# Mamba layer of a three-layer kernel: z's projections, their SiLU, rounding terms and copies in other slots; five buffers for products with C, four each for B and C, C fetched two slots later

## The chip, the cores and the metric

The kernel runs on one core of a Trainium2 chip. TensorE (PE) multiplies matrices into PSUM, VectorE (DVE) does elementwise work and scans, ScalarE (ACT) does activations and copies, GpSimd (POOL) does elementwise work in SBUF, and SyncE (SP) issues most of the DMA transfers. Each engine works through its own instructions in the order in which the program gives them, and waits on semaphores for the others. The metric is the device time of one execution in microseconds (us). The kernel before takes 4107.07 us, the median of 3 runs (4106.33 to 4110.94).

## The reference, cut to what matters

Three layers run one after another on 4096 tokens of 256 channels: a hybrid of convolutions and attention, a bidirectional Mamba layer with a small MLP, and a mixture of experts. The change touches the Mamba layer alone. For each direction (forward, and backward over the reversed tokens) it computes:

```python
xz = einsum('bld,ed->ble', x, in_proj_w);  xc, z = split(xz, 2)      # 512 channels each
xc = silu(depthwise_conv4(xc) + conv_b)
x_dbl = einsum('bld,ed->ble', xc, x_proj_w)                          # dt: 16, B: 16, C: 16
dt = softplus(einsum('blr,dr->bld', dt, dt_proj_w) + dt_proj_b)
h_t = exp(dt_t * A) * h_{t-1} + dt_t * B_t * xc_t                    # 512 channels x 16 states
y_t = sum_s h_t[s] * C_t[s]
y = (y + xc * Dp) * silu(z)
out = y @ out_proj_w.T
```

Forward and backward are added, normalised, put through a leaky MLP, and added to the input; a second LayerNorm makes the input of the third layer.

## The kernel before, in words

**Chunks and slots.** The 4096 tokens are cut into 8 pieces of N = 512. Each piece is worked on once per direction, which makes 16 *chunks* i = 0 to 15; even i is forward (d = 0), odd i is backward (d = 1). A chunk is worked through in 32 *slots* (`SPS`): a slot (e, k, j) holds 128 partitions by 2 x 512 values, that is 64 channels with four of their 16 states each. Within a chunk the slot's number is at = 8e + 2k + j/2, with e = 0..3 (a quarter of the channels), k = 0..3 (a quarter of the states), j = 0 or 2. All 512 slots go through the loop at L2022.

**What a slot does.** In the loop's order, for slot n:

- POOL: `inflow(n + 2)` (L1928) multiplies dt·xc by B into a tile `dbx` (three buffers).
- ACT: `keep(n - 1)` (L1977) copies the last state of the scan before; `decay(n + 1)` (L1918) makes exp(dt·A) for the next slot in a PSUM tile `da` (two buffers), with two activations; `bring(n + 1)` (L1971) adds the state brought in from the chunk before to the next `dbx`. For slots 1, 9, 17 and 24 (`LONG`) POOL does that (L1969).
- DVE: `recur(n)` (L1941) is the scan h = da·h + dbx over 1024 values, and `readout(n)` (L1951) at the end of the slot multiplies the result by C into a tile `h` (pool `hp`, four buffers).
- In seven slots, `POOLED` = {0, 4, 8, 12, 16, 20, 28}, the scan writes straight into a buffer of `h`, and the product with C is made by POOL one slot later (`pooled(n - 1)`, L1956), so DVE has no readout there.
- PE: `sum_states` (L1986) sums `h` over the states into a PSUM tile `y`, for two slots (a pair) at once. A pair that begins at an even slot m is summed in slot m + 2, or in slot m + 3 where m is in `POOLED`. That sum is what sets the pair's two buffers of `h` free.
- DVE: `close` (L1995), in slots 1, 9, 17 and 25, multiplies y by silu(z).

**What runs beside it.** `prepare(q)` is a Python generator that makes chunk q's inputs during the chunk before (from slot 27 of the one before that); one step of it is taken in each slot. In a steady chunk its steps fall so: in slots 3 to 7 the convolution; slot 8 the SiLU of xc with a table load on either side (L1392, and L1331 in `exp_and_log`); slot 9 the projection to dt, B and C (L1398); slot 10 its copy `xd` (L1402) and the write to `bcd`; slots 11 to 15 the projection of dt (L1423) with Abs and Relu (L1419, L1420); slot 16 an Exp; from slot 17 the softplus by quarters: `rounding(e)` (two ACT operations, L1432 and L1433), `total(e)` (PE, L1438), `logs(e)` (ACT Ln, L1441), a last matmul (L1471), `keep_dt(e)` (ACT copy, L1444); and in slots 21, 23, 25, 27 `dt_piece` (POOL, L1496, then two DMA writes of dt and dt·xc, L1500). z is made by `z_of(q, e)` (PE, L1342, four matmul instructions for each e) and copied from PSUM by `keep_z(q, e)` (ACT, L1486): quarters 0 and 1 in slots 9 to 11, quarters 2 and 3 in slots 19 to 22. All these PE results share two PSUM buffers (`mm`). z's SiLU (L2062, two activations between two table loads) comes in slot 0 of the chunk that uses it.

`tail(c)` is another generator, for the LayerNorms and the MLP of two finished chunks. It begins in slot 3 of an even chunk and takes at most one step a slot; each step says which engine it needs next (`needs`), and slots listed for that engine in `FULL` are passed over. So `FULL` sets in which slots the tail's work falls, over the next two chunks.

**Loads.** SP issues, in the order of the loop, `load_bc(i + 1, k)` in slots 24, 26, 28 and 30 (L1529: B and C of quarter k, 256 KB each, spread over the partitions from DRAM, in tiles `b` and `c` of pool `bcp`, five buffers each) and `load_dt` (L1539: dt and dt·xc, 512 KB each) in slots 3, 5, 11, 13, 19, 21, 27 and 29 for the e that follows. The tail's LayerNorms write and read small rows through DRAM on the same queue (L138, L140, L145, L146).

Of the kernel before, what the change touches and what calls it, by code (L numbers as in the profile page):

```python
# [30 lines left out]
NCH = NT // N  # L31
# [6 lines left out]
ET = DI // P  # L38
DS = 16
DR = 16  # L40
SQ = DS // 4
# [1214 lines left out]
def mamba_phase(cx, early, w_in, w_x, w_out, w1, w2, x1d, ud, bcd, dtd, x2d, u2d, usum):  # L1256
# [11 lines left out]
    nc, tc = cx.nc, cx.tc  # L1268
    with ExitStack() as ctx:
        one = ctx.enter_context(tc.tile_pool(name="c_one", bufs=1))  # L1270
        pr = ctx.enter_context(tc.tile_pool(name="c_pr", bufs=2))
        sp = ctx.enter_context(tc.tile_pool(name="c_sp", bufs=1))
        bcp = ctx.enter_context(tc.tile_pool(name="c_bc", bufs=5))
        dtp = ctx.enter_context(tc.tile_pool(name="c_dt", bufs=3))
        up = ctx.enter_context(tc.tile_pool(name="c_u", bufs=3))
        hp = ctx.enter_context(tc.tile_pool(name="c_h", bufs=4))
        ip = ctx.enter_context(tc.tile_pool(name="c_i", bufs=2))
        tl = ctx.enter_context(tc.tile_pool(name="c_tl", bufs=1))
        pda = ctx.enter_context(tc.tile_pool(name="c_pda", bufs=2, space=PSUM))
# [12 lines left out]
        for d in range(2):  # L1292
            for lst, have, src, shape, nm in (
# [6 lines left out]
                t_ = one.tile(shape, FP, name=f"{nm}{d}")  # L1300
# [59 lines left out]
        def prepare(q):  # L1360

            d, got = q % 2, gots[q]

            ps = in_pair(q, 0)
            yield
            yield
            xp = early.wide("xp")
            nc.scalar.copy(xp[:, :, 0:3], halo[d])
            for v in range(2):
                nc.scalar.copy(xp[:, v, 3:], ps[v])  # L1370
            ps = in_pair(q, 2)
            yield
            yield
            for v in range(2):
                nc.scalar.copy(xp[:, 2 + v, 3:], ps[v])
            nc.scalar.copy(halo[d], xp[:, :, N : N + 3])
            for _ in range(4):
                yield

            xc = None  # L1380
            for e in range(ET + 1):
                if e > 0:
                    xc = got["xc"] = xc or pr.tile([P, ET, N], FP, name="xc", tag="xc")
                    nc.scalar.activation(xc[:, e - 1, :], ps, AF.Identity, bias=cx.col(f"convb{d}", e - 1))
                if e < ET:
                    ps = mm_psum()
                    for k in range(4):
                        nc.tensor.matmul(  # L1388
                            ps, taps[d][:, 4 * e + k, :], xp[:, e, k : k + N], start=k == 0, stop=k == 3
                        )  # L1390
                yield
            nc.scalar.activation(xc, xc, AF.Silu)  # L1392
            exp_and_log()
            yield
            ps = mm_psum()
            nx = DR + 2 * DS
            for e in range(ET):
                nc.tensor.matmul(ps[0:nx, :], wx[d][:, e, :], xc[:, e, :], start=e == 0, stop=e == ET - 1)  # L1398
            z_of(q, 0)
            yield  # L1400
            xd = few()[0:nx, :]
            nc.scalar.copy(xd, ps[0:nx, :])  # L1402
            keep_z(q, 0)
            z_of(q, 1)

            at = 0 if d else DR
            nc.sync.dma_start(out=bcd[q], in_=xd[at : at + 2 * DS, :])
            yield


            r = slice(32 * d, 32 * d + DR)
            ex = dt = None
            for e in range(ET + 1):
                if e == 0:
                    keep_z(q, 1)
                if e > 0:
                    ex = early.wide("ex")[:, :, 0:N] if e == 1 else ex
                    dt = got["dt"] = dt or sp.tile([P, ET, N], FP, name="dt", tag="dt")
                    nc.scalar.activation(ex[:, e - 1, :], ps, AF.Abs, bias=cx.col(f"dtb{d}", e - 1))  # L1419
                    nc.scalar.activation(dt[:, e - 1, :], ps, AF.Relu, bias=cx.col(f"dtb{d}", e - 1))  # L1420
                if e < ET:
                    ps = mm_psum()
                    nc.tensor.matmul(ps, wdt[r, P * e : P * e + P], xd[r, :], start=True, stop=True)  # L1423
                yield

            nc.scalar.activation(ex, ex, AF.Exp, scale=-1.0)
            yield
            rds, sums = {}, {}

            def rounding(e):  # L1430
                rds[e] = few()
                nc.scalar.activation(rds[e], ex[:, e, :], AF.Identity, scale=-1.0, bias=-1.0)  # L1432
                nc.scalar.add(rds[e], rds[e], 1.0)  # L1433

            def total(e):
                sums[e] = mm_psum()
                for v, x in enumerate((rds.pop(e), ex[:, e, :], dt[:, e, :])):
                    nc.tensor.matmul(sums[e], cx.ident, x, start=v == 0, stop=False)  # L1438

            def logs(e):  # L1440
                nc.scalar.activation(ex[:, e, :], ex[:, e, :], AF.Ln, bias=1.0)  # L1441

            def keep_dt(e):
                nc.scalar.copy(dt[:, e, :], sums[e])  # L1444
                if q < 2:
                    return
                h = e // 2
                if e % 2 == 0:
                    firsts[q, h] = ip.tile([P, 2], FP, name="first", tag="first")
                nc.scalar.copy(firsts[q, h][:, e % 2 : e % 2 + 1], sums[e][:, 0:1])  # L1450
                if e % 2:
                    first_rows[q, h] = cx.rows.tile([P, 2], FP, name="first_row", tag="first_row", bufs=2)
                    nc.sync.dma_start(out=first_rows[q, h], in_=firsts[q, h])

            rounding(0)
            yield
            for e in range(ET + 1):
                if e > 0:
                    keep_dt(e - 1)
                if e < ET:  # L1460
                    total(e)
                if e < ET - 1:
                    rounding(e + 1)
                if 0 < e < 3:
                    keep_z(q, e + 1)
                yield
                if e < ET:
                    logs(e)
                    if e < 2:
                        z_of(q, e + 2)  # L1470
                    nc.tensor.matmul(sums[e], cx.ident, ex[:, e, :], start=False, stop=True)  # L1471
                if e > 0:
                    dt_piece(q, 1, e - 1)
                if e == 1 and q + 1 < 2 * NCH:
                    load_u(q + 1)
                if e == ET and q > 1:
                    load_first(q, 0)
                yield

        def z_of(q, e):  # L1480
            zs[e] = in_proj(q % 2, gots[q]["u"], ET + e)

        def keep_z(q, e):
            if e % 2 == 0:
                gots[q].setdefault("z", []).append(sp.tile([P, 2, N], FP, name="z", tag="z", bufs=3))
            nc.scalar.copy(gots[q]["z"][e // 2][:, e % 2, :], zs.pop(e))  # L1486
# [33 lines left out]
                old = state[q % 2].rearrange("p (e a b) k -> p e a b k", a=2, b=2)[:, tiles, :, 1, :]  # L1520
                nc.gpsimd.tensor_tensor(brought[q, h], brought[q, h], old, ALU.mult)

        def load_bc(i, k):

            tiles = []
            for nm, r in (("b", 0), ("c", DS)):
                t_ = bcp.tile([P, N], FP, name=nm, tag=nm)
                rows = bcd[i][r : r + DS, :].rearrange("(s k) n -> k s n", s=4)[k]
                nc.sync.dma_start(out=t_, in_=rows[None].to_broadcast([32, 4, N]))  # L1529
                tiles.append(t_)  # L1530
            bcs[i, k] = tiles

        def load_dt(i, e, j):

# [373 lines left out]
        gots, bcs, dts, m_of, das, us, ys, hs = {}, {}, {}, {}, {}, {}, {}, {}  # L1908
# [25 lines left out]
        def recur(n):  # L1934
# [3 lines left out]
            h = hs[n] = hp.tile([P, 2, N], FP, name="h", tag="h")  # L1938
            if n % SPS in POOLED:
                das[n] = h  # L1940
# [52 lines left out]
        def close(i, e):  # L1993
# [4 lines left out]
        CARRY = {30: (0, 0), 31: (0, 2), 9: (1, 0), 11: (1, 2)}  # L1998


        POOLED = {0, 4, 8, 12, 16, 20, 28}

        AHEAD = 5

# [1 line left out]
        LONG = {1, 9, 17, 24}  # L2006

        FULL = {
            "PE": {1, 2, 3, 4, 5, 6, 7, 9, 18, 20, 21, 22, 24, 27, 29},
            "ACT": {0, 6, 7, 8, 9, 14, 15, 16, 20, 22, 30, 31},  # L2010
            "POOL": {1, 5, 9, 13, 17, 21, 23, 25, 27, 29, 30, 31},
            "DVE": {8, 11, 16, 24},
            "DMA": {},
        }
        needs = ["PE"]
        with tc.manual_schedule(engines=ORDERED):
# [5 lines left out]
            for n, (i, e, k, j) in enumerate(slots):  # L2022
                at = n % SPS
# [8 lines left out]
                    decay(n + 1)  # L2032
                bring(n + 1)
                recur(n)
                nxt = (i, e + 1) if e < ET - 1 else (i + 1, 0)
                if nxt[0] < 2 * NCH:
                    if e == ET - 1 and j == 0:
                        load_bc(i + 1, k)
                    if (k, j) == (1, 2):
                        load_dt(*nxt, 0)  # L2040
                    if (k, j) == (2, 2):
                        load_dt(*nxt, 2)
# [11 lines left out]
                if 1 <= at <= 3 and out is not None:  # L2054
                    step(out)
                    if at == 3:
                        out = None
                        if (i - 1) % 2:
                            tails.append(tail((i - 1) // 2))
                if at == 0 and i > 0:  # L2060
                    for z in gots[i]["z"]:
                        nc.scalar.activation(z, z, AF.Silu)  # L2062
                    exp_and_log()
                if i == 0:
# [376 lines left out]
```

## Time and profile before

| | us |
|---|---|
| median of 3 runs | 4107.07 |
| the profiled execution: device time | 4108.35 |
| the profiled execution: span of its instructions | 4106.5 |
| Mamba's scans: first starts, last ends | 1930.3, 3815.0 |
| DVE busy, whole span | 3456.2 (84%) |
| PE busy, whole span | 3577.7 (87%) |
| ACT busy, whole span | 2640.9 (64%) |
| POOL busy, whole span | 1814.7 (44%) |
| between 2000 and 3700 us (1700 us): DVE, POOL, PE, ACT busy | 1579.3, 1457.6, 1422.4, 1294.4 |

The profiled execution lies 1.28 us above the median, and its device time 1.85 us above its span. The profile lists for each line of the kernel the instructions it made, their mean duration, and the engine's idle time just before them with what ended it. `da`, `h`, `dbx`, `y`, `z`, `mm` and so on are tile names. A chunk's beginning can be read from the timeline as the start of its first scan: chunk 5 begins at 2521.3 us, chunk 6 at 2641.7, chunk 7 at 2755.0, chunk 8 at 2877.4. Below, "slot 5.12" is slot 12 of chunk 5.

### The profile page before, as it was taken

The numbers are of one execution on the slowest core, as the hardware profiler recorded it, in microseconds if no ns is written. First come the engines' busy times: TensorE is split into PE (matmuls) and PEld (weight loads), VectorE is DVE, ScalarE is ACT, GpSimd is POOL, SyncE is SP. The second block draws the span as 40 slices with busy tenths as digits, with TensorE's granted clock in tenths as the row PEclk, the third lists the DMA queues.
The fourth block names the chain that finished last, engine by engine and source line by source line (L and its number), as shares of the span: only waits on it lengthen the run. The fifth ranks groups of instructions, "written<-read, shape, count | busy, mean of one in ns | idle before, by whom it ended". The sixth has DMA issues, their size and how long they took to land. (4 is left out here: it accounts for less than half of the span.)

```text
span 4106.5 us, 43589 instructions
## 1 busy us (share of the span) xinstructions
PE 3577.7 (87%) x14968; PEld 1200.4 (29%) x14968; DVE 3456.2 (84%) x2887; ACT 2640.9 (64%) x4233; POOL 1814.7 (44%) x1193
## 2 busy tenths in 40 slices
PE   6769888999999999997788888888888988786898
PEld 2224332222222222222222223222322323222344
DVE  8998777989889889877899999998999999899322
ACT  1111226888888888875678777787877778775222
POOL 3020000000000000002888888888888889898100
PEclk9889998999999999998889999898999989897999
DMA  6232215223222323214333344434334334432121
GB/s 208 94 103 92 80 58 158 51 61 64 66 61 57 66 63 65 50 41 143 121 101 117 113 132 121 136 121 122 109 103 136 122 124 132 132 113 88 56 63 55
DMA packets 164325, 399.95 MB, mean 97 GB/s; under 512 B 36997, under 2 KB 46469, under 8 KB 163838
## 3 DMA queue, kind: packets, MB, share of 16 engines
q1 hardware_dynamic: 137166, 304.26, 23.9%
q0 software_dynamic: 24624, 84.43, 8.9%
q10 hardware_dynamic: 2304, 8.39, 0.6%
q8 instruction: 119, 1.95, 0.2%
q14 instruction: 112, 0.92, 0.1%
HBM read 268.17 MB, written 79.56 MB: 85 GB/s over the span
## 5 line engine op out<-in xcount | busy, mean ns | idle before, releaser
L1928 POOL TENSOR_TENSOR dbx<-dtxr,b 128x1024 f32<-128x1024 f32 x512 | 1202.6, 2358 | 225.5 <-DMA dtxr<-dtd 99.5
L1044 ACT ACTIVATE e<-sc 128x1024 f32<-128x1024 f32 x1024 | 993.7, 1023 | 165.5 <-PE sc L1037 143.0
L1941 DVE TENSOR_TENSOR_SCAN da<-da,state,dbx 128x1024 f32<-128x1024 f32 x400 | 938.9, 2347 | 58.5 <-ACT dbx L1971 17.4
L954 DVE TENSOR_TENSOR s<-s,e 128x1024 f32<-128x1024 f32 x768 | 880.2, 1216 | 19.7 <-ACT e L1044 19.0
L1918 ACT ACTIVATE da<-dtr,aneg 128x512 f32<-128x512 f32 x1024 | 707.9, 691 | 34.5 <-DMA dtr<-dtd 3.1
L1037 PE MATMUL sc<-q,kS 32*128 32x512 f32 x4096 | 648.7, 646 | 15.7 <-ACT e L1044 11.4
L961 PE MATMUL av<-e,vT 128*32 128x512 f32 x4096 | 551.8, 609 | 0.1
L1951 DVE TENSOR_TENSOR h<-da,c 128x1024 f32<-128x1024 f32 x400 | 488.5, 1221 | 22.9 <-PE mm L1423 1.4
L977 POOL DMA_DIRECT2D s<-s x94 | 81.5, 874 | 942.3 <-DVE s L954 856.8
L462 PE MATMUL cv<-v,u 128*128 128x512 f32 x928 | 413.5, 606 | 28.3 <-DVE pad L283 14.2
L1986 PE MATMUL y<-h,sel 128*32 128x512 f32 x2048 | 335.8, 629 | 95.0 <-DVE h L1951 77.2
L1037 PEld LDWEIGHTS sc<-q,kS 32*128 32x128 f32 x4096 | 211.0, 184 | 455.8 <-issue 254.0
L1941 DVE TENSOR_TENSOR_SCAN h<-da,state,dbx 128x1024 f32<-128x1024 f32 x112 | 262.5, 2343 | 53.6 <-PE y L1986 44.1
L1956 POOL TENSOR_TENSOR h<-h,c 128x1024 f32<-128x1024 f32 x112 | 263.9, 2357 | 28.9 <-ACT state L1977 28.8
L1342 PE MATMUL mm<-u,win 128*128 128x512 f32 x464 | 237.7, 654 | 30.7 <-ACT xp L1370 28.1
L462 PEld LDWEIGHTS cv<-v,u 128*128 128x128 f32 x928 | 179.1, 195 | 260.5 <-issue 228.1
L560 DVE SCALAR_TENSOR_TENSOR acc<-pad,wdw_s,acc 128x768 f32<-128x768 f32 (+1 forms) x192 | 235.9, 1233 | 19.9 <-ACT acc L553 14.2
L1977 ACT COPY state<-da 128x2 f32<-128x2 f32 x399 | 63.1, 158 | 280.8 <-DVE h L1951 279.4
L1388 PE MATMUL mm<-xp,taps 128*128 128x512 f32 x480 | 214.1, 598 | 0.0
L143 POOL TENSOR_TENSOR ln_few<-ln_few,minus_half 128x4 f32<-128x4 f32 x29 | 32.1, 1106 | 398.4 <-DMA ln_few<-ln_row 259.5
L954 DVE TENSOR_TENSOR s<-e 128x1024 f32<-128x1024 f32 x128 | 152.0, 1217 | 59.2 <-ACT e L1044 50.3
L961 PEld LDWEIGHTS av<-e,vT 128*32 128x32 f32 x4096 | 81.7, 108 | 394.4 <-issue 386.7
(381 smaller groups left out, 3910.8 us busy)
## 6 DMA issues: line engine op xcount, KB each, us to landing
dtr<-dtd SPq DMA_DIRECT2D x128, 512.0 KB
dtxr<-dtd SPq DMA_DIRECT2D x128, 512.0 KB
s<-s POOLq DMA_DIRECT2D x94, 512.0 KB, 6.0
b<-bcd SPq DMA_DIRECT2D x64, 256.0 KB
c<-bcd SPq DMA_DIRECT2D x64, 256.0 KB
dtd<-dt SPq DMA_DIRECT2D x64, 256.0 KB
dtd<-few SPq DMA_DIRECT2D x64, 256.0 KB
u<-uv SPq DMA_DIRECT2D x24, 640.0 KB
```

Source lines behind the costliest of these rows:

```text
L462: nc.tensor.matmul(rows4(ps), u[:, dy, P * ci : P * ci + P], v[:, dy : dy + HR, ci, :], start=dy + ci == 0, stop=dy == k - 1 and ci == CT - 1,
L954: nc.vector.tensor_tensor(z, x, y, ALU.add)
L961: nc.tensor.matmul(g.av[32 * h : 32 * h + 32, :], vT[:, kb, P * t + 32 * h : P * t + 32 * h + 32], es[h // 2][:, h % 2, :], start=kb == 0, ...
L1037: nc.tensor.matmul(ps[h // 2][:, h % 2, :], kS[r, t, P * kb : P * kb + P], q_t[r, t, :], start=True, stop=True,)
L1044: nc.scalar.activation(e, ps[i], AF.Exp)
L1342: nc.tensor.matmul(ps, win[d][:, t, P * e : P * e + P], u[:, t, ::-1] if d else u[:, t, :], start=t == 0, stop=t == CT - 1,)
L1918: nc.scalar.activation(da[:, v, :], dts[i, e, j][0][:, v, :], AF.Exp, scale=aneg[i % 2][:, a : a + 1])
L1928: nc.gpsimd.tensor_tensor(u, dts[i, e, j][1], bcs[i, k][0][:, None, :].to_broadcast([P, 2, N]), ALU.mult)
L1941: nc.vector.tensor_tensor_scan(das[n].rearrange("p v n -> p (v n)"), da.rearrange("p v n -> p (v n)"), u.rearrange("p v n -> p (v n)"), st ...
L1951: nc.vector.tensor_tensor(hs[n], das[n], bcs[i, k][1][:, None, :].to_broadcast([P, 2, N]), ALU.mult)
L1956: nc.gpsimd.tensor_tensor(hs[n], hs[n], bcs[i, k][1][:, None, :].to_broadcast([P, 2, N]), ALU.mult)
L1986: nc.tensor.matmul(ys[i, e][32 * j : 32 * j + 32, :], cx.sel, hs[n + j // 2][:, j % 2, :], start=False, stop=k == SQ - 1,)
```

## The change

It moves work between slots and changes three counts of buffers; no operation is added or taken away.

- `hp` (products with C) has five buffers instead of four; `bcp` has four of B and four of C instead of five each.
- C of quarter k is fetched two slots after B: in slots 26, 28 and 30, and in slot 0 of the chunk itself for k = 3.
- z's quarter 0 is projected in slot 15 and kept in 17, quarter 1 projected in 17 and kept in 18 (before: 9, 10, 10, 11); quarters 2 and 3 are kept in slots 21 and 23, after that slot's logarithm (before: 20 and 22).
- `rounding(2)` moves from slot 20 to slot 19.
- z's SiLU for chunk i + 1 comes in slot 28 of chunk i instead of slot 0 of chunk i + 1.
- `POOLED` has 10 instead of 0. `FULL` lists other slots, so that the tail's steps fall elsewhere.

```diff
-        bcp = ctx.enter_context(tc.tile_pool(name="c_bc", bufs=5))
+        bcp = ctx.enter_context(tc.tile_pool(name="c_bc", bufs=4))
-        hp = ctx.enter_context(tc.tile_pool(name="c_h", bufs=4))
+        hp = ctx.enter_context(tc.tile_pool(name="c_h", bufs=5))
...
                 nc.tensor.matmul(ps[0:nx, :], wx[d][:, e, :], xc[:, e, :], start=e == 0, stop=e == ET - 1)
-            z_of(q, 0)
             yield
             xd = few()[0:nx, :]
             nc.scalar.copy(xd, ps[0:nx, :])
-            keep_z(q, 0)
-            z_of(q, 1)
...
             for e in range(ET + 1):
-                if e == 0:
-                    keep_z(q, 1)
...
                     nc.tensor.matmul(ps, wdt[r, P * e : P * e + P], xd[r, :], start=True, stop=True)
+                else:
+                    z_of(q, 0)
                 yield
...
             rounding(0)
+            keep_z(q, 0)
+            z_of(q, 1)
             yield
             for e in range(ET + 1):
                 if e > 0:
                     keep_dt(e - 1)
                 if e < ET:
                     total(e)
-                if e < ET - 1:
+                if e == 0 or e == 2:
                     rounding(e + 1)
-                if 0 < e < 3:
-                    keep_z(q, e + 1)
+                if e == 0:
+                    keep_z(q, 1)
                 yield
                 if e < ET:
                     logs(e)
+                    if 0 < e < 3:
+                        keep_z(q, e + 1)
                     if e < 2:
                         z_of(q, e + 2)
                     nc.tensor.matmul(sums[e], cx.ident, ex[:, e, :], start=False, stop=True)
+                if e == 0:
+                    rounding(2)
...
-        def load_bc(i, k):
-
-            tiles = []
-            for nm, r in (("b", 0), ("c", DS)):
+        def load_bc(i, k, which="bc"):
+
+            for nm in which:
+                r = DS * (nm == "c")
                 t_ = bcp.tile([P, N], FP, name=nm, tag=nm)
...
-        POOLED = {0, 4, 8, 12, 16, 20, 28}
+        POOLED = {4, 8, 10, 12, 16, 20, 28}
...
-            "PE": {1, 2, 3, 4, 5, 6, 7, 9, 18, 20, 21, 22, 24, 27, 29},
-            "ACT": {0, 6, 7, 8, 9, 14, 15, 16, 20, 22, 30, 31},
-            "POOL": {1, 5, 9, 13, 17, 21, 23, 25, 27, 29, 30, 31},
-            "DVE": {8, 11, 16, 24},
+            "PE": {1, 2, 3, 4, 5, 6, 7, 8, 9, 10, 15, 18, 19, 20, 21, 22, 24, 27, 29},
+            "ACT": {6, 7, 8, 9, 16, 17, 18, 19, 22, 28, 29, 31},
+            "POOL": {5, 9, 11, 13, 17, 21, 23, 25, 27, 29, 30, 31},
+            "DVE": {1, 9, 11, 17, 25},
...
                 recur(n)
+                if at == 0 and i > 0:
+                    load_bc(i, SQ - 1, "c")
...
                     if e == ET - 1 and j == 0:
-                        load_bc(i + 1, k)
+                        load_bc(i + 1, k, "b")
+                        if k > 0:
+                            load_bc(i + 1, k - 1, "c")
...
-                if at == 0 and i > 0:
-                    for z in gots[i]["z"]:
+                if at == 28 and i + 1 < 2 * NCH:
+                    for z in gots[i + 1]["z"]:
                         nc.scalar.activation(z, z, AF.Silu)
                     exp_and_log()
```

More of the change, by code (lines that the diff above doesn't have):

```diff
@@ L1529, in load_bc @@
                 nc.sync.dma_start(out=t_, in_=rows[None].to_broadcast([32, 4, N]))
-                tiles.append(t_)
-            bcs[i, k] = tiles
+                bcs.setdefault((i, k), []).append(t_)
         def load_dt(i, e, j):
```

## The prediction

> **What bounds the kernel now.** I read the page's busy shares first, then the engines in the steady stretch of the Mamba layer, then what the scan waits for, then the timeline around the longest waits.
>
> ```profile
> DVE  8998777989889889877899999998999999899322
> 2000.00:3700.00 1700.00, 1422.37 (x4162) 482.76 (x4166) 1579.26 (x956) 1294.40 (x2614) 1457.61 (x816) 0.92 0.40 121
> ```
>
> The second line is the view by windows: PE, PEld, DVE, ACT and POOL busy. In slices 20 to 37 DVE is the fullest engine: 1579 of 1700 us. Its work there (512 scans, 400 readouts, the closes, the tail's share) is the same after the change, since `POOLED` keeps seven slots. So the time can only change by DVE's idle time, 121 us in that stretch, and by the ends of the phase. The list of the scan's own waits (line L1941) names most of it:
>
> ```profile
>   PE y L1986: 44.1, 24
>   ACT da L1918: 20.1, 18
>   ACT dbx L1971: 18.2, 19
>   ACT state L1977: 14.5, 14
>   POOL dbx L1969: 9.8, 6
>   POOL dbx L1928: 4.2, 3
> ```
>
> Adding up the gaps before DVE's instructions by slot, over the timeline: `PE y` stands before the scans of slots 8 (9.1 us), 12 (25.0), 16 (2.9), 20 (3.9), and 3.2 in chunk 15; slot 10 has 7.9 (ACT); slots 1 and 2 26.2 (POOL 9.8, ACT 16.4); slots 22 and 24 12.1 (ACT); the tail's `usum` in slot 29 5.5 (POOL); chunk 0 some 18 of its own. Per chunk, from 1 on, odd ones idle some 10 us and even ones 6.6, about 1 us of it in gaps of 0.1 us that stay. Two mechanisms make the rest. The first, in chunk 5, slots 10 to 12 (DVE):
>
> ```profile
> 2557.45 2.36 DVE L1941 TENSOR_TENSOR_SCAN da<-da,state,dbx 128x1024 f32<-128x1024 f32 x1 [1.06 <-ACT state L1977]
> 2561.49 2.35 DVE L1941 TENSOR_TENSOR_SCAN da<-da,state,dbx 128x1024 f32<-128x1024 f32 x1
> 2563.87 1.23 DVE L1951 TENSOR_TENSOR h<-da,c 128x1024 f32<-128x1024 f32 x1
> 2568.75 2.35 DVE L1941 TENSOR_TENSOR_SCAN h<-da,state,dbx 128x1024 f32<-128x1024 f32 x1 [3.66 <-PE y L1986]
> ```
>
> The last scan writes an `h` buffer. With four buffers it needs h(8) back, whose pair POOL multiplies and PE sums only in slot 11, behind z's eight matmuls and the tail's. The second mechanism, at the start of chunk 8 (ACT, and DVE's scan of slot 2):
>
> ```profile
> 2877.50 0.16 ACT L1977 COPY state<-da 128x2 f32<-128x2 f32 x1 [0.58 <-DVE h L1951]
> 2877.69 1.42 ACT L1918 ACTIVATE da<-dtr,aneg 128x512 f32<-128x512 f32 x2
> 2879.13 1.28 ACT L2062 ACT_TABLE_LOAD   x1
> 2880.42 2.00 ACT L2062 ACTIVATE z<-z 128x1024 f32<-128x1024 f32 x2
> 2882.44 1.28 ACT L1331 ACT_TABLE_LOAD   x1
> 2883.74 0.20 ACT L1977 COPY state<-h 128x2 f32<-128x2 f32 x1
> 2883.84 1.41 ACT L1918 ACTIVATE da<-dtr,aneg 128x512 f32<-128x512 f32 x2
> 2885.18 0.28 ACT L1971 ACTIVATE dbx<-dbx,brought 128x1 f32<-128x1 f32 x1
> 2885.50 2.36 DVE L1941 TENSOR_TENSOR_SCAN da<-da,state,dbx 128x1024 f32<-128x1024 f32 x1 [1.82 <-ACT state L1977]
> ```
>
> ACT can begin a slot's work only when the scan before is read out, at the scan's start. A SiLU group (4.6 us with its loads) put into a slot therefore sets the scan two slots on at 8.1 us after the slot's start (2877.38 to 2885.50). Unhindered, a slot takes DVE 3.52 us with its readout and 2.26 without; a close adds 0.46, a tail step of 512 values 0.5 to 0.65.
>
> **The change, part by part.**
>
> *Five buffers of h.* A pooled slot n now needs h(n - 5), of a pair that is summed by slot n - 3 at the latest (pair 10 in slot 13, for slot 15's readout; pairs 6, 14 in slots 8, 16 for 12, 20). Against that, PE is late by at most 5.9 us in the waits seen, under two slots. All 44.1 us go. What is late next is ACT: **-44.1**.
>
> *The SiLU of xc in slot 8* stays, and what hid part of it goes. Slot 8 is pooled, so the scan of slot 10 comes at 8.0 us after slot 8 (chunk 6: 2670.8 to 2678.8) against 2.26 + 3.52 + 0.46 = 6.25 for DVE. Today the wait in slot 8 gives ACT a start, and the tail's DVE steps (1.0 in slot 9 of even chunks, 0.65 in slot 8 of odd) fill the rest; both leave. 14 chunks x 1.75 = 24.5 against 7.9 now: **+16.6**.
>
> *z's SiLU from slot 0 to slot 28.* Slots 1 and 2 lose their 26.2. Slot 28 is pooled too, with no close after it, and ACT has one bring more (0.1): the scan of slot 30 comes at 8.22 against 5.79, or 6.44 in even chunks with a leaky step: 7 odd x 2.44 + 7 even x 1.79 + chunk 0 2.3 = 31.9. Left in slot 1 of even chunks, where POOL waits for dt·xc (rival A): I take 0.5 x 7 = 3.5. Together **+9.2**.
>
> *The softplus slots.* Effective ACT times, start to next start when nothing waits: base of a slot 1.72, rounding 1.19, keep_z 0.47, logs 0.52, keep_dt 0.52. Slots 20 and 22 lose 1.66 and 0.47; slots 17 to 19 gain 0.47, 0.47 and 1.19, slots 21 and 23 0.47 each. Followed slot by slot, ACT enters slot 20, which is pooled, 0.1 us late in odd chunks and 0.8 in even ones (there with the tail's copy in 17), so slot 21's scan waits 0.4 in even chunks. In slots 21 to 23 PE's z3 now stands behind keep_z(2) and delays the last sum, and keep_dt(1) waits 1.1 for it; with the tail's two scalings (0.71 each, now in slot 23) slot 25 waits 0.35. 7 x 0.75 = 5.3 against 12.1: **-6.8**.
>
> *The tail's other slots.* The same steps. `usum` falls in slot 4, one slot after POOL's product instead of right behind it: **-5.5**. Its PE work leaves slots 8 to 10 and 15. It ends some seven slots later, before the next tail's first allowed slot (11), so it costs nothing; if it ran over, a whole tail step of 0.65 to 1.2 us would be added to DVE's critical slots, not to its work.
>
> *Pooled 10 for 0.* POOL has three products with C in slots 9, 11 and 13: 8 x 2.36 = 18.9 us with its inflows of slots 8 to 12, against 16 to 17 of DVE time in slots 8 to 12. It falls 2 to 3 us behind; an inflow has some 4 us of lead (needed two slots on), so nothing: cover gone, each us beyond is a us per chunk, 14. In slot 0 the readout (1.14) comes back to DVE, and leaves slot 10, after its wait: even.
>
> *B and C.* B's buffer is free after POOL's inflow two slots ahead, and SP has by then waited for that slot's `dt_piece` (L1500) behind it. C waits for the readouts of slots 25, 27, 29, as three of four C loads do now, and for 31; its first reader is six slots later (over 18 us; the longest landing seen at a boundary is 9, dt·xc issued at 2396.6 and used at 2405.8). Zero; 256 KB less stand ahead of slot 29's load. If C came late, readout would wait for it on DVE itself.
>
> *Chunk 0.* Less POOL work in slot 1 (2.36) against ACT's added 2.1 in slots 17 to 19: from -3 to +3, I take 0.
>
> Sum: -44.1 + 16.6 + 9.2 - 6.8 - 5.5 = **-30.6**. From 4108.35 that is 4077.8, and from the median, 1.28 lower, some **4076**. Differences under 0.2% (8 us) are about what measurement can't tell from none.
>
> The Trainium skill speaks against a table load next to a critical slot: "ScalarE: Activation LUTs", section "What ACT_TABLE_LOAD costs", has a drain of some 1.38 us on top of the load's 1.28. By that, as an estimate, each of z's 15 SiLU groups would take 2.8 us more in its new place, and the sum would be near +10. The rows above show 1.28 and the activation 1.29 after the load's start, and no drain.
>
> **The rivals.**
>
> *A. SP holds back dt: slower.* In odd chunks the tail's second row now goes through DRAM in slot 27, ahead of the B of slot 28 and the dt of slot 29 on SP. SP's waits show the price:
>
> ```profile
> SPq L146 <- DMA ln_inv<-ln_few: 33.0, 13, 5.6
> SPq L140 <- DMA ln_row<-ln_rstd: 24.8, 13, 3.6
> ```
>
> Slot 1's scan already waits up to 2.6 us for that dt·xc. Against it: slot 0 is 1.26 us longer now, slot 30 starts later, and a blocked queue empties. From 30.6 / 7 = 4.4 us per even chunk on the gain is gone; at 5.6 it is +9 us: 4116.
>
> *B. ACT and PE pass the wait on.* In chunk 5 ACT too was late at slot 12 (Abs waited 2.8 us for PE). If PE is still late there, half of the 25 us returns, and the softplus slots keep their 12: -11, 4096. For it: PE is 84% busy. Against: slots 9 to 11 lose eight matmuls of z (3.7 us) and one down-projection.
>
> *C. More is hidden.* Slots 10 and 30 find ACT ahead (as in chunk 6's slot 10, 0.4), half of their 56 us is filled by DVE's other steps: -58, 4049. Against: those steps were moved away.
>
> **How the numbers follow.** Forecast, gain 20 to 42: 0.6 (own range 4064 to 4087). B 0.17, C 0.1, A 0.13 (in 0.08 of it slower, in 0.05 within 0.2%). B's end within 0.2%: 0.03. So faster 0.84, same 0.08, slower 0.08. The range 4053 to 4098 leaves out A's upper part and C's end.
>
> **What would show it.** `PE y` gone from the scan's waits; some 1.75 us before slot 10 and 1.8 to 2.4 before slot 30 in every chunk, by ACT; slots 1 and 2 nearly free; DVE busy unchanged. I am wrong if slot 1's wait grows past 3 us, if `h` or readouts wait for PE or for `c`, or if POOL's inflow becomes the scan's releaser in slots 12 to 16.

## The result, and the profile after

| | before | after |
|---|---|---|
| median, us | 4109.00 (4106.33 to 4110.98, 4 runs) | 4157.55 (4151.21 to 4164.48, 4 runs) |
| ratio after to before, 95% interval | | 1.0119 (1.0096 to 1.0142) |
| the profiled execution: device time, span, us | 4108.35, 4106.5 | 4151.21, 4149.3 |
| Mamba's scans: first start, last end, length, us | 1930.3, 3815.0, 1884.7 | 1930.8, 3856.4, 1925.6 |
| DVE, ACT, POOL busy, whole span, us | 3456.2, 2640.9, 1814.7 | 3457.1, 2640.9, 1817.6 |

The change makes the kernel 1.2% slower, by 48.5 us; 4076 was forecast, and the range ended at 4098. The profiled execution is the fastest of the four. In it the scans take 40.9 us longer, and the rest of the kernel stays where it was to within 2 us. DVE has the same work, so the time is DVE's idle time, as the prediction had argued. The profile's slices of DVE, and the busy times between 2000 and 3700 us (PE, PEld, DVE, ACT, POOL):

```profile
DVE  8988787889889889778898989998999899899422
```

```profile
2000.00:3700.00 1700.00, 1405.98 (x4070) 471.36 (x4068) 1536.46 (x928) 1261.56 (x2541) 1419.60 (x790) 0.90 0.36 116
```

DVE is busy for 1536 us of that stretch instead of 1579, so it idles 43 us more. Two lists of the profile name the new waits: what the scan waited for, and below the dots who waited for the scan. Each line gives the engine, the tile that the other instruction writes and its line, then us in total and number of times:

```profile
its engine sat idle before it (us, times) until:
  ACT dbx L1973: 64.0, 44
  ACT da L1920: 54.9, 41
  ACT state L1979: 31.5, 15
  POOL dbx L1930: 0.2, 1
...
  ACT da L1920: 73.3, 41
```

`PE y`, 44.1 us before, is gone, as forecast. All that is left, but for 0.2 us, is ACT. The last line is the surprise: ACT's `decay` (L1920, the exponential into `da`) itself waited 41 times, 73.3 us, for a scan. In before the same view has:

```profile
  ACT da L1918: 1.9, 1
```

DVE waits for ACT, and ACT waits for DVE.

Chunk 5 shows around slots 8 to 10 which scan that is. The timeline of DVE, with the scans of slots 8, 9 and 10:

```profile
2561.71 2.34 DVE L1943 TENSOR_TENSOR_SCAN h<-da,state,dbx 128x1024 f32<-128x1024 f32 x1
2565.59 2.36 DVE L1943 TENSOR_TENSOR_SCAN da<-da,state,dbx 128x1024 f32<-128x1024 f32 x1 [1.54 <-ACT da L1920]
...
2571.79 2.35 DVE L1943 TENSOR_TENSOR_SCAN h<-da,state,dbx 128x1024 f32<-128x1024 f32 x1 [2.14 <-ACT state L1979]
```

and of ACT at the same place:

```profile
2561.83 0.16 ACT L1979 COPY state<-da 128x2 f32<-128x2 f32 x1 [0.69 <-DVE h L1953]
2564.09 1.42 ACT L1920 ACTIVATE da<-dtr,aneg 128x512 f32<-128x512 f32 x2 [2.10 <-DVE h L1943]
2565.52 1.28 ACT L1392 ACT_TABLE_LOAD   x1
2566.81 1.91 ACT L1392 ACTIVATE xc<-xc 128x2048 f32<-128x2048 f32 x1
```

ACT is free at 2561.99, and slot 7 has been read out by then. By the prediction's rule it could make `da` of slot 9 at once. It starts at 2564.09, when the scan of slot 8 (2561.71 + 2.34 = 2564.05) has ended, and the scan of slot 9 then waits for it. The built program, which gives each tile its address, says why: there the `da` of slot 9 lies in the same place in PSUM as the `da` of slot 8. `da` comes from a pool of two buffers, and I had taken them to alternate. They do so in before, except in three slots (9, 13 and 17 of chunk 0). In after 45 of the 512 tiles got the place of the tile just before: slot 9 in 15 chunks, slot 21 in 15, slot 17 in 7, slot 5 in 6, and slots 11 and 13 once each. All of these follow a pooled slot, in which the scan writes into `h` and is thus the last reader of its `da`.

DVE's idle time in chunks 1 to 14, added up from the timeline by slot (us):

| slots | before | after |
|---|---|---|
| 8, 12, 16, 20 (PE's sum) | 41.8 | 0.9 |
| 1, 2 (z's SiLU, POOL) | 27.0 | 0.2 |
| 10 (SiLU of xc in slot 8) | 8.2 | 29.8 |
| 30 (z's SiLU in slot 28) | 0.7 | 30.2 |
| 5, 9, 17, 21 (`decay` waits for the pooled scan) | 2.8 | 69.0 |
| 3 (the sum of the layer's output waits for PE) | 0.2 | 3.0 |
| 29 (`usum`) | 6.3 | 1.5 |
| 22 to 25 (softplus) | 16.9 | 17.3 |
| all others | 12.3 | 10.4 |
| sum | 116.2 | 162.3 |

The fifth row is the whole loss and more. So the first theory after the result, called P in the expectations, was that the reuse of a PSUM buffer made the change slow. Its rival, called Q there, was that the moved work overloads ACT in these slots, and that the buffer only shows where ACT is late.

### The profile page after: what moved, and what is told of

Same layout as the page of the kernel before. It is cut to its first block, busy times and chain, and to the rows that moved or that the text cites. A ratio compares the mean times of both kernels' runs of the same rounds, so it can differ in the third digit from the quotient of the medians.

```text
span 4149.3 us, 43558 instructions
## 1 busy us (share of the span) xinstructions
PE 3596.6 (87%) x14968; PEld 1198.5 (29%) x14968; DVE 3457.1 (83%) x2887; ACT 2640.9 (64%) x4233; POOL 1817.6 (44%) x1193
## 5 line engine op out<-in xcount | busy, mean ns | idle before, releaser
L1920 ACT ACTIVATE da<-dtr,aneg 128x512 f32<-128x512 f32 x1024 | 708.2, 692 | 103.5 <-DVE h L1943 73.3
L1342 PE MATMUL mm<-u,win 128*128 128x512 f32 x464 | 257.1, 694 | 92.4 <-ACT xp L1370 84.4
L1988 PE MATMUL y<-h,sel 128*32 128x512 f32 x2048 | 302.9, 630 | 34.5 <-POOL h L1958 21.8
L1943 DVE TENSOR_TENSOR_SCAN h<-da,state,dbx 128x1024 f32<-128x1024 f32 x112 | 262.3, 2342 | 30.0 <-ACT state L1979 29.8
```

The costliest lines, as they stand in the source:

```text
L1342: nc.tensor.matmul(ps, win[d][:, t, P * e : P * e + P], u[:, t, ::-1] if d else u[:, t, :], start=t == 0, stop=t == CT - 1,)
L1920: nc.scalar.activation(da[:, v, :], dts[i, e, j][0][:, v, :], AF.Exp, scale=aneg[i % 2][:, a : a + 1])
L1943: nc.vector.tensor_tensor_scan(das[n].rearrange("p v n -> p (v n)"), da.rearrange("p v n -> p (v n)"), u.rearrange("p v n -> p (v n)"), st ...
L1988: nc.tensor.matmul(ys[i, e][32 * j : 32 * j + 32, :], cx.sel, hs[n + j // 2][:, j % 2, :], start=False, stop=k == SQ - 1,)
```

## The experiments

Each run is set against runs of before on the same chip. Those medians lie between 4107.87 and 4114.36, and the start of the scans lies between 1920.7 and 1941.0 in the profiles, so the table also gives the length of the scans (from the first one's start to the last one's end, one profile each), which leaves out what varies ahead of them.

| run | median, us | ratio to before (95%) | length of the scans | idle, chunks 1 to 14 |
|---|---|---|---|---|
| before | 4107.87 to 4114.36 | 1 | 1884.7 | 116.2 |
| after | 4157.55 | 1.0119 (1.0096 to 1.0142) | 1925.6 | 162.3 |
| e1 after, `da` alternating | 4088.21 | 0.9946 (0.9931 to 0.9962) | 1856.6 | 97.3 |
| e2 before, `da` alternating | 4111.67 | 1.0007 (0.9986 to 1.0027) | 1881.6 | 113.0 |
| e3 before, buffer counts alone | 4186.24 | 1.0197 (1.0164 to 1.0229) | 1955.6 | some 181 |
| e4 the same, `da` alternating | 4178.16 | 1.0173 (1.0146 to 1.0200) | 1949.2 | 174.3 |
| e5 the same, C two slots later | 4094.52 | 0.9968 (0.9955 to 0.9982) | 1866.0 | 100.6 |
| e6 e1 with the old `FULL` | 4101.29 | 0.9981 (0.9961 to 1.0001) | 1874.9 | 107.8 |
| e7 e1, z's SiLU in slot 0 | 4054.46 | 0.9872 (0.9847 to 0.9897) | 1827.8 | 70.8 |
| e8 before, reuse put in | 4165.79 | 1.0150 (1.0121 to 1.0179) | 1932.7 | 161.7 |
| e9 e1 with four buffers of `h` | 4086.07 | 0.9937 (0.9914 to 0.9961) | 1859.8 | 96.2 |
| e10 e7, slot 24 pooled for slot 8 | 4092.89 | 0.9950 (0.9929 to 0.9970) | 1858.9 | 101.3 |
| e11 e7, two tail steps in slots 8 and 9 | 4053.43 | 0.9857 (0.9834 to 0.9880) | 1821.4 | 62.8 |

**e1: the changed kernel with `da` in two buffers by parity.** Nothing but the place of `da` is different:

```diff
-            da = das[n] = pda.tile([P, 2, N], FP, name="da", tag="da")
+            da = das[n] = pda.tile([P, 2, N], FP, name="da", tag=f"da{n % 2}", bufs=1)
```

(The two tiles that share this pool at the end of the layer, `wide` and `pv`, take `da0` and `da1`.)

> The changed kernel, with the two PSUM buffers of da fixed by the slot's parity (even slots one, odd slots the other). In the built program of the changed kernel 45 of 512 da tiles got the same buffer as the tile one slot before, in slots 5, 9, 17 and 21, right after a scan of a pooled slot; in the kernel before 3 did. Theory P (the loss is this reuse: the decay for slot n + 1 must wait for the scan of slot n): the waits before slots 5, 9, 17, 21, some 63 us over chunks 1 to 14, go, and slot 10's fall from 2.1 to 1.75 us each; 4151 less 63 less 5 gives about 4083 (4075 to 4096). Theory Q (ACT is overloaded in these slots by the moved roundings and copies and z's SiLU, and the buffer only shows where it is late): the waits move to the next scan, 4140 to 4165.

4088.21: 69.3 us faster than after, in the scans' length 69.0 us. The line of `decay` in the list of costliest groups (busy, mean ns, then the idle time before it) in after:

```profile
L1920 ACT ACTIVATE da<-dtr,aneg 128x512 f32<-128x512 f32 x1024 | 708.2, 692 | 103.5 <-DVE h L1943 73.3
```

and in e1:

```profile
L1920 ACT ACTIVATE da<-dtr,aneg 128x512 f32<-128x512 f32 x1024 | 708.2, 692 | 31.8 <-DMA dtr<-dtd 2.0
```

The same 1024 instructions at the same 692 ns, without the wait for the scan. ACT at slot 8 of chunk 5, where the scan of slot 8 runs from 2553.09 to 2555.43:

```profile
2554.23 0.15 ACT L1979 COPY state<-da 128x2 f32<-128x2 f32 x1
2554.41 1.42 ACT L1920 ACTIVATE da<-dtr,aneg 128x512 f32<-128x512 f32 x2
2555.84 1.28 ACT L1392 ACT_TABLE_LOAD   x1
```

`decay` now begins while that scan runs, and it has left the list of those who waited for the scan. The scan's own waits shrink to these:

```profile
  ACT dbx L1973: 30.7, 26
  ACT state L1979: 29.0, 15
  ACT da L1920: 20.3, 22
```

Slots 5, 9, 17 and 21 together fall from 69.0 to 8.8 us. Slots 10 and 30 keep 27.3 and 30.2. P holds; Q would have had the waits move to the next scan.

**e2: before with `da` by parity.** The same edit on before, to see whether it is worth anything by itself.

> The kernel before with da's buffers fixed by parity, and nothing else. Theory P: 3 slots of 512 change, at 1.5 us each at most: 4103 to 4110, the same as before. Theory Q: the same. If fixing the buffers gains more here, or costs something, then what e1 shows is not the reuse alone.

No difference is seen (1.0007, 0.9986 to 1.0027): before had three reuses to lose. So e1's gain is not a merit of the edit but the removal of what the change had brought in.

**e8: before with the reuse put in.** The counter-test: `da`'s buffer is made to repeat in slots 9 and 21 of every chunk, 32 times, and nothing else is touched.

```diff
-            da = das[n] = pda.tile([P, 2, N], FP, name="da", tag="da")
+            da = das[n] = pda.tile([P, 2, N], FP, name="da",
+                                   tag=f"da{(n + 2 * (n // SPS) + (n % SPS >= 9) + (n % SPS >= 21)) % 2}", bufs=1)
```

> The kernel before, where the da tiles of slots 9 and 21 of every chunk are made to take the same PSUM buffer as the tile of the slot before, and nothing else. Theory P: each of these 32 decays waits for the pooled scan's end, 2.3 us after its start, and the next scan comes 1.5 us late, less what the tail's step in slot 8 of odd chunks hides (0.65); with slot 10 behind it, 4108 + 35 to 50, so 4140 to 4160. Theory Q (a late buffer is taken up by the slack of ACT and DVE): 4105 to 4115.

4165.79 against 4111.73, 54 us slower, some 6 us more than P's range allowed; the scans' length grows by 48.0. The view of those who waited for the scan has ACT's `decay` again:

```profile
  ACT da L1918: 72.4, 31
```

Slots 9 and 21 take 17.7 and 25.1 us (before: 0 and 1.5). Slot 10, which follows the late table loads, takes 22.1 instead of 8.2. Thirty-two tiles that share a buffer are enough for a loss of the size measured, in a kernel that has no other part of the change.

**e3 and e4: the buffer counts alone, without and with alternating `da`.** Before with five buffers of `h` and four each of B and C; C is still fetched with B.

```diff
-        bcp = ctx.enter_context(tc.tile_pool(name="c_bc", bufs=5))
+        bcp = ctx.enter_context(tc.tile_pool(name="c_bc", bufs=4))
-        hp = ctx.enter_context(tc.tile_pool(name="c_h", bufs=4))
+        hp = ctx.enter_context(tc.tile_pool(name="c_h", bufs=5))
```

> The kernel before with five buffers of h and four each of B and C, and nothing else of the change. In its built program 17 da tiles share the buffer of the slot before, 15 of them in slot 9. Theory P: the 44 us of waits for PE before the pooled scans go, slot 10 takes 5 us more, and slot 9 gives back 15 x 1.5 us, part of it hidden by the tail's steps there: about 4108 - 39 + 20 = 4089 (4080 to 4100), with a new wait of the scan of slot 9 for ACT da. Theory Q: the waits for PE go and nothing new comes: 4069 (4060 to 4078).

> As e3, with da's buffers fixed by parity. Theory P: 4108 - 44 + 5 = 4069 (4060 to 4080), 15 to 25 us under e3. Theory Q: the same as e3.

Both missed widely: 4186.24 and 4178.16, where 4089 and 4069 were expected. The reuse (17 tiles in e3's program, 15 of them in slot 9) is little of it: the two medians lie 8 us apart, with intervals that overlap, and slot 9 falls from 17.7 us in e3 to 6.3 in e4. In e4 the waits for PE's sum are gone as expected, but the scan waits elsewhere:

```profile
  POOL dbx L1969: 52.7, 16
  ACT dbx L1971: 46.3, 44
  ACT da L1918: 27.0, 24
  ACT state L1977: 22.6, 15
```

The first line is slot 1: POOL adds the brought-in state there late, in every chunk, because its inflow waits for dt·xc (139.0 us in all, 99.5 in before). SP's queue (us in total, times, longest) has the reason, at the load of B and C:

```profile
SPq L1529 <- DVE h L1951: 130.7, 50, 4.8
```

In before that line has 0.5 us in two times. With four buffers of C the load issued in slot 24 needs the C that slot 25's readout still reads, and the queue stands still until then, with the dt of the next chunk behind it. That this is the cause, e5 tests.

**e5: e4 with C fetched two slots later.** The change's own edit of the loads, on top of e4:

```diff
+                if at == 0 and i > 0:
+                    load_bc(i, SQ - 1, "c")
...
-                        load_bc(i + 1, k)
+                        load_bc(i + 1, k, "b")
+                        if k > 0:
+                            load_bc(i + 1, k - 1, "c")
```

> The kernel before with five buffers of h, four each of B and C, C fetched two slots later, and da's buffers fixed by parity; z, its SiLU, the roundings, POOLED and FULL as before. Run e4 lost some 70 us against the ledger, most of it before the scans of slots 0 and 1 (POOL late with dbx). Theory S (four buffers of C that are fetched with B block SP in slots 24 to 30 until C's last readout, and dt's loads stand behind): the waits of slots 0 and 1 fall from 68 us to the 26 of before, 4178 less 42 or more gives 4100 to 4136. Theory P alone (the h term of the prediction holds whole): 4108 - 44 + 10, 4065 to 4085. Theory T (e4's loss comes from the fifth buffer of h, not from C): unchanged, 4165 to 4185.

4094.52: 84 us faster than e4, so the late load of C makes up for what four buffers cost. It is some 6 us better than the best that theory S allowed, and does not reach what P alone would give. SP's wait for readouts, and the scan's waits:

```profile
SPq L1529 <- DVE h L1950: 78.4, 20, 6.5
```

```profile
  ACT state L1976: 24.8, 22
  ACT dbx L1970: 22.9, 19
  ACT da L1917: 19.1, 14
```

SP still waits 78.4 us for readouts, but slots 0 and 1 now take 3.0 us instead of 71.7: here the queue's wait costs the scan nothing that the profile shows. Against before the gain is 17 us (18.7 in the scans' length), not 44. Slots 8, 12, 16 and 20 fall from 41.8 us to 0, but slot 13 rises from 1.9 to 21.5: there a subtraction of the tail waits for PE, 3.4 us in every odd chunk from 3 to 13, where slot 12 had waited 3.7 before (5.9 in chunk 7). Slot 10 rises by 4.2 and slot 22 by 5.5. So PE was late itself; a fifth buffer lets DVE run on by one slot, to the next instruction that needs PE.

**e6: e1 with before's `FULL`.** Here the tail's steps fall where they fell before.

```diff
-            "PE": {1, 2, 3, 4, 5, 6, 7, 8, 9, 10, 15, 18, 19, 20, 21, 22, 24, 27, 29},
-            "ACT": {6, 7, 8, 9, 16, 17, 18, 19, 22, 28, 29, 31},
-            "POOL": {5, 9, 11, 13, 17, 21, 23, 25, 27, 29, 30, 31},
-            "DVE": {1, 9, 11, 17, 25},
+            "PE": {1, 2, 3, 4, 5, 6, 7, 9, 18, 20, 21, 22, 24, 27, 29},
+            "ACT": {0, 6, 7, 8, 9, 14, 15, 16, 20, 22, 30, 31},
+            "POOL": {1, 5, 9, 13, 17, 21, 23, 25, 27, 29, 30, 31},
+            "DVE": {8, 11, 16, 24},
```

> The changed kernel with da's buffers fixed and the tail's slots (FULL) of before. By the prediction's ledger the tail's DVE steps again fill part of the waits of slot 10 (0.65 to 1.0 us in each chunk, 11 us) and of slot 30 in odd chunks (7 us), and usum waits again (5 us): 4088 less 13 gives 4075 (4066 to 4084). If the tail's PE work in slots 8 to 13 is what FULL had to move (theory B: it delays Abs and the sub in slot 13), 4095 or more.

4101.29, 13 us slower than e1 (18 in the scans' length), where the ledger had made it 13 faster; the second expectation held. Slot 13 waits for PE again (14.0 us against 0.3 in e1) and slot 7 takes 7.7 (2.4 in e1), while slots 10 and 30 keep more cover (21.6 and 23.4 against 27.3 and 30.2). The new `FULL` takes the tail's PE work away from slots 8, 10 and 15, and as a whole (its other lists change too) it is worth more than the cover which leaves with it.

**e9: e1 with four buffers of `h`.** Is the fifth buffer still worth anything once z's matmuls and the tail's PE work have left slots 9 to 11?

```diff
-        hp = ctx.enter_context(tc.tile_pool(name="c_h", bufs=5))
+        hp = ctx.enter_context(tc.tile_pool(name="c_h", bufs=4))
```

> The changed kernel with da's buffers fixed and four buffers of h instead of five. If the fifth buffer is what takes the 44 us of waits for PE away, as the prediction's first term has it: waits for PE y come back before the scans of slots 8, 12, 16 and 20, and 4088 becomes 4115 to 4135. If PE is in time anyway, because z's matmuls and the tail's PE work left slots 8 to 11: 4088 to 4098. Slot 12, now with 10 and 8 pooled before it, can wait more than before.

The ratios of the two kernels to before are 0.9937 (0.9914 to 0.9961) and, in e1, 0.9946 (0.9931 to 0.9962): not to be told apart. The scans' waits in e9:

```profile
  ACT dbx L1973: 27.7, 19
  ACT state L1979: 19.6, 15
  PE y L1988: 15.8, 14
  ACT da L1920: 15.6, 9
```

`PE y` is back with 15.8 us, in slots 8 and 20, but not the 25 us of slot 12; and while DVE waits in slot 8, ACT gets ahead, so slot 10 falls from 27.3 to 17.8. One wait pays for the other: all idle time together is 96.2 against 97.3.

**e7: e1 with z's SiLU back in slot 0.** The rest of the change stays, among it that slot 0 is no longer pooled.

```diff
-                if at == 28 and i + 1 < 2 * NCH:
-                    for z in gots[i + 1]["z"]:
+                if at == 0 and i > 0:
+                    for z in gots[i]["z"]:
```

> The changed kernel with da's buffers fixed and z's SiLU back in slot 0, which has its readout now. The 27 us before slot 30 go; the scan of slot 2 comes 8.1 us after slot 0's start against 3.52 + 3.98 = 7.5 for DVE, 0.6 x 15 = 9: 4088 less 18 gives 4070 (4062 to 4080). If POOL's late dbx (dt's load at the chunk's border) sets slots 1 and 2 instead: 4080 to 4095.

4054.46: 34 us faster than e1 (28.8 in the scans' length), and 1.3% faster than before; the best that was expected was 4062. The scan's waits:

```profile
  ACT state L1979: 35.0, 25
  ACT da L1920: 13.4, 15
  ACT dbx L1973: 4.3, 13
  POOL dbx L1971: 3.3, 4
  POOL dbx L1930: 2.2, 2
```

Slot 30 falls from 30.2 to 1.5 us; slots 1 and 2 rise from 0.2 to 12.7, not to the 27.0 of before. The same two SiLU activations with the same two loads cost less than half there. The expectation's reason is that slot 0 now keeps its readout on DVE, which gives ACT 3.5 us instead of 2.3 to work beside; it put 9 us before slot 2, and 9.3 are there. No run changes that readout alone.

**e10: e7 with slot 24 pooled in place of slot 8.** If a table load costs little beside a slot with its readout on DVE, slot 8 should get its readout back as well.

```diff
-        POOLED = {4, 8, 10, 12, 16, 20, 28}
+        POOLED = {4, 10, 12, 16, 20, 24, 28}
```

> Run e7 with POOLED 24 instead of 8, so that slot 8, where xc's SiLU stands on ACT, keeps its readout. Slot 10's scan comes 8.0 us after slot 8 against 3.52 + 3.98 = 7.5 for DVE: its wait falls from 1.7 to 2.1 us to about 0.6, 14 x 1.25 = 17: 4054 less 17 is 4037 (4030 to 4047). If POOL, which has dt_piece and a product with C in slots 21, 25 and 29 then, falls more than its lead of 4 us behind: 4054 to 4075, with waits for POOL dbx in slots 24 to 28.

Slot 10 did what was expected (25.9 us in e7, 9.2 here), yet the kernel is 38 us slower than e7 (31 in the scans' length), beyond both expectations. The scan's list begins with:

```profile
  POOL dbx L1971: 22.9, 11
  ACT dbx L1973: 22.7, 22
```

Slot 1 waits 22.7 us for POOL (3.4 in e7), in the even chunks above all. POOL in turn waits there for the load of dt·xc: in the even chunks from 4 on its inflow for slot 1 starts 3.1 to 5.1 us after the chunk's first scan, in e7 at most 2.1 after it. Slot 25 takes 12.3, but there the scan waits for ACT, 1.75 us in each even chunk from 2 on; ACT makes the tail's two scalings there beside slot 24, which has lost its readout. That the load of dt·xc comes later is shown; that the third pooled product among slots 20, 24 and 28 makes it late, by putting POOL behind where it makes dt·xc (slots 21 to 27), is argued only.

**e11: e7 with the tail's first two steps (the mean on PE, the subtraction on DVE) let into slots 8 and 9 of even chunks**, the subtraction as cover for the SiLU of xc.

```diff
-                if tails and (i == 2 * NCH - 1 or at not in FULL[needs[0]]):
+                if tails and (i == 2 * NCH - 1 or at not in FULL[needs[0]] or (i % 2 == 0 and at in (8, 9))):
```

> Run e7 with the tail's first two steps in slots 8 and 9 of even chunks (mean, sub) instead of 11 and 12; odd chunks keep the changed slots. The sub (1.0 us of DVE time) then stands in slot 9, where DVE waits for ACT, in 7 chunks: 4054 less 7 is 4047 (4042 to 4052). If the mean's matmuls hold up PE's projection in slot 9: no gain or a loss, 4054 to 4062.

4053.43, ratio 0.9857 (0.9834 to 0.9880). Slot 10 falls from 25.9 to 16.4 us, the scans' length by 6.4 in one profile each; by their ratios to before e7 and e11 are not to be told apart. Either beats both kernels of this case.

## Why the prediction was wrong

**The step that failed** is the premise under all the ACT terms: "ACT can begin a slot's work only when the scan before is read out, at the scan's start." As the whole condition that holds as long as `da` alternates between its two buffers. The changed program puts 45 tiles into the buffer of the slot before, and there ACT can begin `decay` only at the scan's end, 2.3 us later. The sum had no such term. It measures 69 us (after against e1), and 48 to 54 with 32 such tiles put into before alone (e8). No rival named it. From -30.6 the sum becomes +38; measured were +40.9 in the scans' length and +48.5 in the medians. The profile of before held a hint: one `decay` with 1.9 us of waiting for a scan, in chunk 0. I had put that chunk's idle time down as "some 18 of its own" and not asked why a `decay` would wait for the scan beside it. Which buffer a tile gets can be read from the built program, and what the reuse costs is shown by e1 and e8. *Why* the other edits change the buffer stays open; the counts of buffers alone bring 17 of the 45 (e3).

**With that wait taken away the sum comes near, in part by luck.** e1's scans are 28.1 us shorter than before, against -30.6; by its ratio e1 is 22 us below before (15.6 to 28.3), 4088 where 4076 was said. But in chunks 1 to 14, for which the terms make some 30 (without the 3.2 of chunk 15 and the 2.3 of chunk 0), the idle time falls by only 18.9 us (116.2 to 97.3). The other 9 us lie in chunks 0 and 15 (3.8 and 1.7 shorter) and in DVE's work between them, where the sum had put next to nothing. Term by term, idle time in chunks 1 to 14 of e1:

- *Five buffers of h, -44.1.* The idle time of slots 8, 12, 16 and 20 went as said (41.8 to 1.0, and that in a step of the tail), but under the wrong name. With the buffers and the late C alone only 17 us come (e5), since the wait moves to slot 13; without the fifth buffer, in the changed layout, nothing is lost (e9). What lets PE be in time is the changed layout: the new `FULL`, with the tail's PE work in other slots, is worth 13 to 18 us (e6); what share z's matmuls have by leaving slots 9 to 11 was not tested alone. "What is late next is ACT" was wrong where PE work stays: next was PE, at another reader. Rival B had named that mechanism; its condition, PE late in slot 12, did not come about in the changed layout.
- *SiLU of xc, 24.5 in slot 10.* 27.3 (1.7 in even chunks, 2.1 in odd ones, where 1.75 was said). Mechanism right, 2.8 us short. (In chunk 6 of before the scan of slot 8 began at 2671.3; the 2670.8 of the prediction is the end of the readout ahead of it.)
- *z's SiLU in slot 28, 31.9 in slot 30.* 30.2: 1.8 in even chunks and 2.4 in odd, as worked out (1.79 and 2.44). After's timeline of ACT, and the scan of slot 5.30 that waits:

```profile
2637.06 1.42 ACT L1920 ACTIVATE da<-dtr,aneg 128x512 f32<-128x512 f32 x2
2638.41 0.28 ACT L1973 ACTIVATE dbx<-dbx,brought 128x1 f32<-128x1 f32 x1
2638.71 1.28 ACT L2068 ACT_TABLE_LOAD   x1
2640.01 2.00 ACT L2068 ACTIVATE z<-z 128x1024 f32<-128x1024 f32 x2
2642.03 1.28 ACT L1331 ACT_TABLE_LOAD   x1
```

```profile
2645.08 2.36 DVE L1943 TENSOR_TENSOR_SCAN da<-da,state,dbx 128x1024 f32<-128x1024 f32 x1 [2.41 <-ACT dbx L1973]
```

  The scan of slot 28 began at 2636.75, so slot 30 comes 8.33 us after it, where 8.22 was said. Slots 1 and 2 are free: the remainder of 3.5 us that I kept there did not come. What I did not work out is that in the changed kernel, with slot 0 out of `POOLED`, that wait is less than half without any move (12.7 in e7); so the move that I booked inside +9.2 costs 29 to 34 us against leaving SiLU where it was.
- *The softplus slots, -6.8.* Slots 22 to 25 go from 16.9 to 10.8, which is -6.1, and slot 21 takes 2.3 more: -3.8.
- *usum, -5.5.* 6.3 to 1.5: -4.8.
- *Not in the sum:* slot 3, where the addition of the layer's output waits for PE, takes 7.1 us instead of 0.2, 1.0 in each even chunk.
- *Pooled 10 for 0, B and C, at zero.* No `POOL` or DMA release of weight stands in e1's list, and readout waits for no C, though SP waits 79.9 us for readouts in e1, as in e5. The cover that I named for C, a first reader six slots later, was the right one to name; what I did not price is the old place with the new count, where the queue stands still: 84 us (e4 against e5).
- *Rival A*, dt held back by SP, would have shown in slot 1; it is at 0 (in e10 slot 1 does wait for that load). *Rival C*, half of slots 10 and 30 hidden, did not come: 57.5 us remain in them.

Of the signs named to show the forecast wrong (slot 1 past 3 us, waits for PE or C, POOL late in slots 12 to 16) none appeared in after above 0.5 us. The listed signs of it being right did appear (slot 10 at 2.1 us instead of 1.75), and the kernel was still slower: a list of signs covers only the mechanisms that one has thought of.

## What to carry to other kernels

Where the order of two buffers matters, name them by parity, or look in the built program which address each tile got: an edit far away can make a pool hand out the buffer that was just read. In a profile it shows as an engine that waits for a later instruction than the dependences of the source require. A wait for a free buffer is cured by a further buffer only if its releaser is not late for all its other readers; if it is, the next reader waits. And a burst on the helper engine, such as a table load with its activation, belongs beside a slot in which the bound engine has its full work: the same SiLU cost 30 us behind a shortened slot and 13 behind a full one. Shortening another slot instead has its own price: in e10 it ate more than slot 10 gave back.

## What the runs showed of the hardware

In the moved groups the rows above show a table load that takes 1.28 us and little else: the load starts at 2638.71, the SiLU starts at 2640.01, the next load follows its end at 2642.03. A group of load, two SiLUs and load takes 2638.71 to 2643.32, 4.6 us, as in before, so moving it brought no new cost of its own on ACT. The Trainium skill ("ScalarE: Activation LUTs", section "What ACT_TABLE_LOAD costs") counts a drain of some 1.38 us on top of a load's 1.28; in these rows none is to be seen.
